# Edge counts scattered in BF16 under a bound computed on the chip, with an FP32 recount in a branch, and the first graph convolution summed from three BF16 parts

## The chip, the cores and the metric

The kernel runs on one core of a Trainium2 chip, in one launch. The metric is device time in microseconds (us) of that launch. The core has five engines with queues of their own: TensorE (PE, with its weight loads listed as PEld), VectorE (DVE), ScalarE (ACT), GpSimd (POOL) and SyncE (SP), which here issues nearly all plain transfers. GpSimd issues the indirect ones, those that add into memory and those that convert a type. Sixteen DMA engines carry all of them. P is 128, the number of partitions.

## The reference

3,125 nodes with 256 features, 100,000 edges (`src`, `dst`, sorted by `dst`), and 65,536 edges of a second graph (`edge_index` of the mixture stage). What matters here is cut from two layers:

```python
def segment_sum(src, seg, n): return jax.ops.segment_sum(src, seg, n)
xn = layernorm(x)
# layer 0, graph convolution
agg = segment_sum(xn[src], dst, N)
h = (xn + agg) @ W.T + b                        # then batch norm over the nodes
x = x + h_normed + linear_attention_stack(xn)   # four layers
# layer 0, second part: graph attention over edge_index picks experts
x = x + experts(layernorm(x), edge_index)
# layer 1: the same edges src, dst, twice
xn = layernorm(x)
h = (1 + eps1) * xn + segment_sum(xn[src], dst, N)
h = relu(relu(h @ W1a + b1a) @ W1b + b1b)
h = (1 + eps2) * h + segment_sum(h[src], dst, N)
x = x + relu(h @ W2a + b2a) @ W2b + b2b + attention(xn)
x = x + mixture_of_experts(layernorm(x))
```

The kernel writes a segment sum as a matrix product. It counts for every pair of nodes how many edges go from the one to the other, which makes a matrix of 3,125 x 3,125, and multiplies the features by it on TensorE. The matrix of `src`, `dst` is used three times; that of the second graph, C, is used in the graph attention.

## The kernel before

**Counting the edges.** Each edge gets a key, `src * N + dst` as FP32, which is its place in the matrix. 128 edges make a column, one per partition: 782 columns for list a (`src`, `dst`) and 512 for list b (the second graph). The columns are taken in windows: for list a 1, 7 and then 8 columns wide up to column 88, and from there 5 and 4 wide in turn, by chunks of at most 32 columns (`chunks_of`, L236). The last chunk is filled up to whole windows; edges that fill a list carry source 0 and destination N, and BAD = 2^24 is added to their keys.

`Edges.prepare` (L311) works out the values on VectorE. For each column of a window one instruction (L343) compares its keys with all keys of the window; equal keys that stand earlier weigh BEFORE = 4096 and all others 1, and the sum goes into `val`. So the first edge of a key gets the number of edges with that key in the window, and the others get at least 4096. A few short instructions (L353 to L357) then replace by an unused place (`dump`) the index of an edge that is not the first of its key, or that only fills the list. `scatter` (L390) issues one indirect transfer on GpSimd for each column, which adds the 128 values to the matrix in memory. Within a window no place occurs twice, so the program is told that those scatters need not wait for each other (L402), and each scatter of a window waits for those of the window before (L405). `both` (L413) sets the order: from column 88 a window of list a and two columns of list b in turn; what is left of list b, 198 columns in windows of 16 (TAIL), is scattered last. Before that, SP clears both matrices (`clear`, L454): AT for list a, C2 for list b, each in FP32, 25 transfers each.

This is spread over the four attention layers of layer 0: `beside` (L537) lets `both` run on a step after every tile of 128 nodes.

**First graph convolution.** After the layers, xn is loaded again (L700). `aggregate` (L657) goes over the matrix in two passes, of three and of four groups of 512 columns. For each of 25 row tiles SP loads a slice of AT in FP32 (L673), VectorE takes its maximum into `most` (L675), and TensorE multiplies xn by it in FP32 (L680); the first tile also adds xn itself by the identity (L688). `done0` brings the sums to SBUF, multiplies them by the weights and collects batch norm statistics. Beside this, GpSimd still scatters the last columns of list b. The next stage, graph attention, loads C from L880 on.

**The branch flag.** In the graph attention's second pass the maximum is brought together over the partitions, and `more` becomes 1 if it is over MOST = 256 (L923 to L926). In the same pass GpSimd copies AT to A1 in BF16, in 25 transfers spread over the pass (`copy_counts`, L929).

**Layer 1.** Integers to 256 are exact in BF16. `sums` (L1406) multiplies the features, split into three BF16 parts (`parts`, L1397), by A1. For counts over 256 there is `residue` (L1436): for 7 groups of columns and 25 row tiles it loads a slice of AT and of A1, each into a tile with one buffer, forms what A1 lacks in two further BF16 parts with four VectorE operations, and multiplies the three parts of the features by both. It stands in a branch (`if_more`, L1459), once after the first sum (L1595, two blocks of 128 features) and once before the second (L1650, four blocks). A branch is a unit: nothing from inside runs beside what is outside.

Of the kernel before, what the change touches and what calls it, by code (L numbers as in the profile page):

```python
# [17 lines left out]
P = 128  # L18
N = 3125
# [65 lines left out]
def tile_gps(ctx: ExitStack, tc: tile.TileContext, a, out):  # L85
# [207 lines left out]
    class Edges:  # L293
# [7 lines left out]
        def __init__(self, ep, w_before, dump, key, width, used, rows, mat, tag):  # L301
# [7 lines left out]
            self.ps = None  # L309

        def prepare(self, cols, win):  # L311
# [7 lines left out]
            for c in range(c0, c1, win):  # L319
# [20 lines left out]
                for j in range(k):  # L340
                    junk = ep.tile([P, WIDE * P], BF16, name="junk", tag="junk", bufs=2)
# [15 lines left out]
            V.tensor_tensor(idx, rel[:, :w], dump[:, :w], op=OP.add)  # L357
            yield

        def prepare_tail(self, c, k):  # L360
# [9 lines left out]
            for j in range(k):  # L370
                for i, (h, w) in enumerate(halves):
                    junk = ep.tile([P, WIDE * P], BF16, name="junk", tag="junk", bufs=2)
# [17 lines left out]
        def scatter(self, c, end, other=None):  # L390

            if c < self.used:
# [3 lines left out]
                    in_=self.val[:, c:c + 1], in_offset=None, compute_op=OP.add)  # L396
# [16 lines left out]
    def both(ea, eb, clear_b):  # L413
# [36 lines left out]
    with ExitStack() as st:  # L450
# [3 lines left out]
        def clear(mat):  # L454

            m = mat.rearrange("(p b f) -> p b f", p=P, f=CLR // 4)
            for b in range(25):
                nc.sync.dma_start(m[:, 4 * b:4 * b + 4, :], zero[:, None, :].to_broadcast([P, 4, CLR // 4]))
                yield
# [10 lines left out]
        first, later = clear(AT), clear_own()  # L470
# [5 lines left out]
        steps(first, 4)  # L476
        with tc.tile_pool(name="ps_keys", bufs=1, space=PSUM) as ps:
            key_a = keys(ep, ps, a["src"], a["dst"], E0, True, "a")
            steps(first, 3)
# [35 lines left out]
        ea = Edges(ep, w_before, dumpf, *key_a, AT, "a")  # L515
        behind = both(ea, Edges(ep, w_before, dumpf, *key_b, C2, "b"), later)
# [140 lines left out]
    def aggregate(ps, ap, X, nfb, self_id, passes, done, most, shared):  # L657


        for groups in passes:  # L660
            c0, c1 = 512 * groups[0], min(N, 512 * (groups[-1] + 1))
            bank, acc = None, {}
            for i, g in enumerate(groups):
                if g == shared:
                    bank = ps.tile([P, nfb, P], F32, name="agb", tag="agb", bufs=1)
                for fb in range(nfb):
                    acc[fb, i] = (bank[:, fb, :] if g == shared else
                                  ps.tile([P, 512], F32, name=f"ag{fb}_{i}", tag=f"ag{fb}_{i}", bufs=1))
            for s in range(NT):
                r = rows_of(s)  # L670
                ch = ap.tile([P, 512 * 3 + cols_of(NG - 1)], F32, name="ch", tag="ch", bufs=3)
                for q0, q1 in split_rows(r):
                    nc.sync.dma_start(ch[q0:q1, :c1 - c0], AT2[s * P + q0:s * P + q1, c0:c1])  # L673
                at = passes.index(groups) * NT + s
                V.tensor_reduce(most[:r, at:at + 1], ch[:r, :c1 - c0], axis=AX.X, op=OP.max)  # L675
                for fb in range(nfb):
                    w = X[:r, s, fb * P:(fb + 1) * P]
                    for i, g in enumerate(groups):
                        n = cols_of(g)
                        T.matmul(acc[fb, i][:, :n], lhsT=w, rhs=ch[:r, i * 512:i * 512 + n],  # L680
                                 start=s == 0 and (g != shared or fb == 0),
                                 stop=s == NT - 1 and (g != shared or fb == nfb - 1), skip_group_check=g == shared)
                if s == 0:
                    for fb in range(nfb):
                        for i, g in enumerate(groups):
                            for j, t in enumerate(tiles_of(g)):
                                q = rows_of(t)
                                T.matmul(acc[fb, i][:, j * P:j * P + q], lhsT=X[:q, t, fb * P:(fb + 1) * P],  # L688
                                         rhs=self_id[:q, :q], start=False, stop=False, skip_group_check=g == shared)
            for i, g in enumerate(groups):  # L690
                for fb in range(nfb):
                    done(i, g, fb, acc[fb, i], cols_of(g))
# [3 lines left out]
    most_p = ctile([P, 1], "most_p")  # L696
    more = ctile([1, 1], "more", I32)
    with ExitStack() as st:
        gp = st.enter_context(tc.tile_pool(name="gnn0", bufs=1))
        xn = gp.tile([P, NT, D], F32, name="xn", tag="xn")  # L700
        for g in range(NG):
# [1096 lines left out]
```

## Time and profile before

| what | value |
|---|---|
| median of 3 runs | 5,089.27 us (5,079.68 to 5,099.22) |
| the profiled execution's own time | 5,094.23 us |
| its span, first to last instruction | 5,092.4 us |
| PE busy | 4,003.0 us, 79% |
| DVE busy | 3,218.2 us, 63% |
| POOL busy | 2,769.6 us, 54% |
| ACT busy | 1,467.1 us, 29% |
| DMA, mean | 104 GB/s |

The span cut into 40 equal slices shows where which engine is busy; a digit is the share in tenths, and PEclk is the granted TensorE clock in tenths of full speed. A slice is 127 us:

```profile
PE   1457888878766877849979964666689998999999
PEld 1234455445544454524446641222245444544477
DVE  7978887898899874113348996889973031331231
ACT  0311133114111321200014448989740021000033
POOL 0668888888888888877760006888620031001034
PEclk6668888889787878969989986888899999999999
DMA  9954444444332322247656536543291212212266
```

The first 17 or 18 slices are the attention layers with the scatters of the edges on POOL, slices 18 to 21 the first convolution and the batch norm, then up to slice 29 the graph attention, then layer 1 and the experts. The costliest groups are listed by line with the number of instructions, their busy time in us, the mean of one in ns, and the idle time of the engine just before them with what ended it. In order of time, a row has its start and length in us, engine and line, what it writes and reads, and in brackets the idle time before it and what ended that.

### The profile page before, as it was taken

The numbers are of one execution on the slowest core, as the hardware profiler recorded it, in microseconds if no ns is written. First come the engines' busy times: TensorE is split into PE (matmuls) and PEld (weight loads), VectorE is DVE, ScalarE is ACT, GpSimd is POOL, SyncE is SP. The second block draws the span as 40 slices with busy tenths as digits, with TensorE's granted clock in tenths as the row PEclk, the third lists the DMA queues.
The fourth block names the chain that finished last, engine by engine and source line by source line (L and its number), as shares of the span: only waits on it lengthen the run. The fifth ranks groups of instructions, "written<-read, shape, count | busy, mean of one in ns | idle before, by whom it ended". The sixth has DMA issues, their size and how long they took to land. (4 is left out here: it accounts for less than half of the span.)

```text
span 5092.4 us, 48980 instructions
## 1 busy us (share of the span) xinstructions
PE 4003.0 (79%) x16189; PEld 2300.3 (45%) x16189; DVE 3218.2 (63%) x8074; ACT 1467.1 (29%) x2293; POOL 2769.6 (54%) x1860
## 2 busy tenths in 40 slices
PE   1457888878766877849979964666689998999999
PEld 1234455445544454524446641222245444544477
DVE  7978887898899874113348996889973031331231
ACT  0311133114111321200014448989740021000033
POOL 0668888888888888877760006888620031001034
PEclk6668888889787878969989986888899999999999
DMA  9954444444332322247656536543291212212266
GB/s 371 329 117 74 83 72 55 81 79 56 26 26 17 34 16 1 5 88 138 131 101 216 186 123 176 138 121 104 84 280 55 83 50 70 64 54 68 57 170 169
DMA packets 457112, 530.76 MB, mean 104 GB/s; under 512 B 213682, under 2 KB 354779, under 8 KB 451798
## 3 DMA queue, kind: packets, MB, share of 16 engines
q1 hardware_dynamic: 256058, 494.24, 30.7%
q0 software_dynamic: 200784, 33.23, 13.9%
q8 instruction: 133, 2.18, 0.2%
q14 instruction: 137, 1.11, 0.1%
HBM read 397.41 MB, written 169.95 MB: 111 GB/s over the span
## 5 line engine op out<-in xcount | busy, mean ns | idle before, releaser
L394 POOL DMA_INDIRECT AT<-vala,keya x782 | 1232.6, 1576 | 421.0 <-issue 221.0
L394 POOL DMA_INDIRECT C<-valb,keyb x512 | 807.6, 1577 | 203.4 <-issue 143.0
L988 POOL TENSOR_TENSOR ex<-ex,pqb 128x1024 f32<-128x1024 f32 (+3 forms) x200 | 367.0, 1857 | 434.0 <-ACT ex L987 433.4
L343 DVE SCALAR_TENSOR_TENSOR junk<-kr,keya,w_before 128x640 bf16<-128x640 f32 (+2 forms) x729 | 573.1, 830 | 0.6 <-DMA kr<-keys_a 0.6
L383 DVE SCALAR_TENSOR_TENSOR junk<-kr,keyb,w_before 128x1024 bf16<-128x1024 f32 (+1 forms) x390 | 482.3, 1269 | 4.5 <-DMA kr<-keys_b 4.4
L194 PE MATMUL tr<-ident,rows 128*128 128x128 f32 (+1 forms) x500 | 103.4, 361 | 465.8 <-ACT rows L180 441.0
L228 PE MATMUL mm<-hT,w 128*128 128x512 f32 (+1 forms) x896 | 418.2, 632 | 17.2 <-ACT hT L196 16.9
L1430 PE MATMUL ag<-chb,Hb 128*128 128x512 bf16 (+1 forms) x1800 | 420.1, 387 | 13.0 <-DMA chb<-A 13.0
L887 DVE CUSTOM_DVE_ANT_0 am<-asb,pen 128x1664 f32<-128x1664 f32 (+3 forms) x200 | 357.3, 1786 | 51.0 <-ACT pen L884 41.0
L649 PE MATMUL o<-w,hid 128*128 128x256 f32 (+1 forms) x1600 | 383.0, 393 | 0.0
L1023 PE MATMUL pa<-ex,hgp 128*32 128x512 f32 (+3 forms) x1400 | 208.4, 676 | 197.1 <-DVE ex L1011 193.9
L1011 DVE SCALAR_TENSOR_TENSOR ex<-ex,ct 128x2048 f32<-128x2048 f32 (+3 forms) x175 | 345.7, 2007 | 23.4 <-ACT ex L1004 13.8
L1004 ACT ACTIVATE ex<-ex,as 128x1024 f32<-128x1024 f32 (+3 forms) x400 | 345.2, 932 | 3.4 <-DVE ex L993 2.9
L649 PEld LDWEIGHTS o<-w,hid 128*128 128x128 f32 (+1 forms) x1600 | 296.9, 190 | 79.4 <-issue 34.7
L1259 POOL DMA_INDIRECT slots<-rb,r_ati x50 | 49.8, 997 | 516.2 <-DVE rb L1252 407.6
L680 PE MATMUL ag<-ch,xn 128*128 128x512 f32 (+1 forms) x600 | 272.5, 602 | 62.3 <-issue 62.3
L231 ACT ACTIVATE hid<-mm,fm 128x512 f32<-128x512 f32 (+1 forms) x336 | 211.1, 632 | 370.4 <-PE mm L228 353.0
L228 PEld LDWEIGHTS mm<-hT,w 128*128 128x128 f32 x896 | 191.7, 233 | 234.9 <-issue 190.0
L194 PEld LDWEIGHTS tr<-ident,rows 128*128 128x128 f32 (+1 forms) x500 | 66.7, 174 | 506.6 <-ACT rows L180 469.2
L180 ACT ACTIVATE rows<-xs,ln_nmr,rs_y 128x256 f32<-128x256 f32 (+1 forms) x200 | 105.7, 592 | 649.0 <-DVE ln_nmr L173 625.1
L1430 PEld LDWEIGHTS <-Hb 128*128 128x128 bf16 (+1 forms) x2100 | 184.9, 99 | 226.9 <-issue 35.1
L675 DVE TENSOR_REDUCE most<-ch 128x1 f32<-128x1536 f32 (+3 forms) x50 | 89.0, 1780 | 228.7 <-DMA ch<-AT 228.5
(430 smaller groups left out, 6962.5 us busy)
## 6 DMA issues: line engine op xcount, KB each, us to landing
AT<-zero SPq DMA_DIRECT2D x25, 1528.0 KB
C<-zero SPq DMA_DIRECT2D x25, 1528.0 KB
cnt<-C SPq DMA_DIRECT2D x24, 1562.5 KB
cd<-C SPq DMA_DIRECT2D x36, 1024.0 KB
kr<-keys_b SPq DMA_DIRECT2D x64, 512.0 KB
f1w<-in_f_w_dram SPq DMA_DIRECT2D x56, 512.0 KB
slots<-blank SPq DMA_DIRECT2D x15, 1820.0 KB
kr<-keys_a SPq DMA_DIRECT2D x48, 512.0 KB
```

Source lines behind the costliest of these rows:

```text
L228: T.matmul(ph[:, :n], lhsT=w1[:, k, hb * P:(hb + 1) * P], rhs=xT[:, k, :n], start=(k == 0), stop=(k == 1))
L231: S.activation(h[:, :n], ph[:, :n], AF.Gelu, bias=bias[hb])
L343: V.scalar_tensor_tensor(junk[:, :k * P], self.kr[:, at:at + k * P], key[:, c + j:c + j + 1], self.w_before[:, u:u + k * P], op0=OP.is_equ ...
L383: V.scalar_tensor_tensor(out, kk, key[:, c + j:c + j + 1], by, op0=OP.is_equal, op1=OP.mult, accum_out=more[:, j:j + 1] if i else self.val ...
L394: s = G.indirect_dma_start(out=self.flat, out_offset=bass.IndirectOffsetOnAxis(ap=self.idx[:, c:c + 1], axis=0), in_=self.val[:, c:c + 1], ...
L649: T.matmul(po[:r], lhsT=hid[hb][:, j * P:j * P + r], rhs=w2[:, hb, :], start=(hb == 0), stop=False)
L680: T.matmul(acc[fb, i][:, :n], lhsT=w, rhs=ch[:r, i * 512:i * 512 + n], start=s == 0 and (g != shared or fb == 0), stop=s == NT - 1 and (g ...
L887: V.tensor_tensor_reduce(out=junk[:r, :w], in0=asb[:r, h, c0:c1], in1=pen[:r, :w], scale=1.0, scalar=-3.0e38, op0=OP.subtract, op1=OP.max, ...
L988: G.tensor_tensor(e, e, pq[:r, h, :n], op=OP.add)
L1004: S.activation(ex[:r, h, :n], ex[:r, h, :n], AF.Exp, bias=sc)
L1011: V.scalar_tensor_tensor(e4, e4, 1.0, ct[:r, None, :m].to_broadcast([r, 4, m]), op0=OP.min, op1=OP.mult)
L1430: T.matmul(acc[fb, g][:, :n], lhsT=Xb[:r, s, i, fb * P:(fb + 1) * P], rhs=ch[:r, at:at + n], start=first, stop=last, skip_group_check=g == ...
```

## The change

- A1, the matrix in BF16, takes the place of AT in the first counting: it is cleared (in 20 transfers) and list a is scattered into it, from `low`, a BF16 copy of the values that ACT makes in `prepare`.
- For each window of list a, `prepare` takes the largest value under BEFORE into a column of `most`, on each partition. `at_most` takes the maximum over the partitions by two transposes and adds up all windows; `more` is 1 if that is over MOST = 256. It is set before the first convolution.
- If `more` is 1, `recount` clears AT, scatters list a once more in FP32 into it and copies it to A1, and `residue` adds what A1 lacks. For the recount no scatter is declared independent of another.
- The first convolution is done by `sums`, from three BF16 parts of xn; these are made by ACT and, for the differences, TensorE. `sums`, `residue` and `parts` move up in the text. `aggregate`, the maximum over AT and the copies in the graph attention's second pass are removed.
- The last 198 columns of list b are no longer scattered by `both`; they are kept in `tail` and scattered after the branch.
- `junk` has one buffer in place of two. aT starts at zero and is added to.

```diff
         def __init__(self, ep, w_before, dump, key, width, used, rows, mat, tag):
...
+            self.low = None
+            if mat.dtype == BF16:
+                self.low = ep.tile([P, width], BF16, name=f"low{tag}", tag=f"low{tag}")
+                self.most, self.windows = ep.tile([P, 2 * P], F32, name=f"most{tag}", tag=f"most{tag}"), 0
+                V.memset(self.most, 0.0)
         def prepare(self, cols, win):
...
+            if self.low is not None:
+                S.activation(self.low[:, c0:c1], val, AF.Copy)
+                n = w // win
+                V.scalar_tensor_tensor(rel[:, :w], val, BEFORE, val, op0=OP.is_lt, op1=OP.mult)
+                V.tensor_reduce(self.most[:, self.windows:self.windows + n],
+                                rel[:, :w].rearrange("p (n w) -> p n w", w=win), axis=AX.X, op=OP.max)
+                self.windows += n
...
-                    in_=self.val[:, c:c + 1], in_offset=None, compute_op=OP.add)
+                    in_=(self.val if self.low is None else self.low)[:, c:c + 1], in_offset=None, compute_op=OP.add)
...
+        def at_most(self, ps):
+            top = small.tile([P, 2], F32, name="e_top", tag="e_top")
+            for i in range(2):
+                p = ps.tile([P, P], F32, name="mt", tag="mt", bufs=2)
+                T.transpose(p, self.most[:, i * P:(i + 1) * P], ident)
+                V.tensor_reduce(top[:, i:i + 1], p, axis=AX.X, op=OP.max)
+            p = ps.tile([P, P], F32, name="mt", tag="mt", bufs=2)
+            for i in range(2):
+                T.matmul(p[:1, :1], lhsT=top[:, i:i + 1], rhs=ones_col, start=(i == 0), stop=(i == 1))
+            return p[:1, :1]
+        def recount(self, zero, mat, low):
+            f = CLR // 4
+            m = mat.rearrange("(p b f) -> p b f", p=P, f=f)
+            for b in range(25):
+                nc.sync.dma_start(m[:, 4 * b:4 * b + 4, :], zero[:, None, :].to_broadcast([P, 4, f]))
+            for c in range(self.used):
+                G.indirect_dma_start(
+                    out=mat.rearrange("(n o) -> n o", o=1),
+                    out_offset=bass.IndirectOffsetOnAxis(ap=self.idx[:, c:c + 1], axis=0),
+                    in_=self.val[:, c:c + 1], in_offset=None, compute_op=OP.add)
+            for b in range(25):
+                G.dma_start(out=low.rearrange("(p f) -> p f", p=P)[:, CLR * b:CLR * (b + 1)],
+                            in_=mat.rearrange("(p f) -> p f", p=P)[:, CLR * b:CLR * (b + 1)])
...
-                eb.scatter(c, (c - c0) % TAIL == TAIL - 1 or c == eb.made - 1)
+                tail.append((c, (c - c0) % TAIL == TAIL - 1 or c == eb.made - 1))
...
-        ea = Edges(ep, w_before, dumpf, *key_a, AT, "a")
+        ea = Edges(ep, w_before, dumpf, *key_a, A1, "a")
...
+        S.activation(aT, ones_col[:, 0:1, None].to_broadcast([P, 2, N]), AF.Copy, scale=0.0)
...
+            V.tensor_scalar(more, ea.at_most(ps), MOST, None, op0=OP.is_gt)
+            for t in range(NT):
...
+                S.activation(xb[:r, t, 0, :], x, AF.Copy)
+                for i in range(2):
+                    p = ps.tile([P, D], F32, name="rest", tag="rest", bufs=6)
+                    T.matmul(p[:r], lhsT=ident[:r, :r], rhs=x, start=True, stop=False)
+                    for k in range(i + 1):
+                        T.matmul(p[:r], lhsT=less[:r, :r], rhs=xb[:r, t, k, :], start=False, stop=(k == i))
+                    S.activation(xb[:r, t, i + 1, :], p[:r], AF.Copy)
+        with (tc.tile_pool(name="g0t", bufs=1) as rp, tc.tile_pool(name="ps_g0t", bufs=1, space=PSUM) as ps,
+              if_more()):
...
+            ea.recount(zero, AT, A1)
+            residue(ps, rp, xb, 2, add0)
+        for c, end in tail:
+            eb.scatter(c, end)
...
-            aggregate(ps, gp, xn, 2, ident, [[0, 1, 2], [3, 4, 5, 6]], done0, most, NG - 1)
+            sums(ps, gp, xb, 2, [[0, 1, 2], [3, 4, 5, 6]], done0, shared=NG - 1, own=ident_b)
...
-                if s % 3 == 2:
-                    copy_counts(state.get("gone"))
-                    state["gone"] = o
```

More of the change, by code (lines that the diff above doesn't have):

```diff
@@ L469, in tile_gps @@
         V.memset(each, 1.0)
-        first, later = clear(AT), clear_own()
+        first, later = clear(A1), clear_own()
         def steps(it, n):
@@ L1459, in if_more @@
-    def if_more():
-        return tc.If(nc.values_load(more[0:1, 0:1], min_val=0, max_val=1,
-                                    skip_runtime_bounds_check_because="the result of a comparison") > 0)
     with ExitStack() as st:
```

190 lines of the change are left out of this document (80 added, 110 removed).

## The prediction

> **What bounds the kernel now.** I read the page's costliest groups first, then the busy time by stretches, then GpSimd in order of time where the first graph stage begins.
>
> ```profile
> L394 POOL DMA_INDIRECT AT<-vala,keya x782 | 1232.6, 1576 | 421.0 <-issue 221.0
> L394 POOL DMA_INDIRECT C<-valb,keyb x512 | 807.6, 1577 | 203.4 <-issue 143.0
> L680 PE MATMUL ag<-ch,xn 128*128 128x512 f32 (+1 forms) x600 | 272.5, 602 | 62.3 <-issue 62.3
> ```
>
> Until 2,250 us GpSimd scatters edges, 1.58 us each and one after the other: the two lists together hold it for 2,040 us of busy time. In the stretch 1,950 to 2,100 us it is busy 125.5 of 150 us, which is 81 scatters, one per 1.86 us. The layers' own work ends at 2,197 us and the first aggregation (L680) waits until 2,260 for the last scatter.
>
> ```profile
> 2243.92 1.55 POOL L394 DMA_INDIRECT AT<-vala,keya  x1 [0.30 <-issue]
> 2247.45 1.55 POOL L394 DMA_INDIRECT AT<-vala,keya  x1 [1.97 <-DMA AT<-vala,keya]
> 2249.31 1.55 POOL L394 DMA_INDIRECT C<-valb,keyb  x1 [0.30 <-issue]
> 2251.17 1.55 POOL L394 DMA_INDIRECT C<-valb,keyb  x1 [0.30 <-issue]
> ```
>
> The second line is the one to keep: the last scatter of list a may not run beside the one before it, and starts 3.53 us after it (2247.45 - 2243.92) where its neighbours follow in 1.86.
>
> **The question that decides: is the branch taken?** Before, `more` compared the largest real count with 256; the largest is 3, and the residue's lines (L1446 to L1457) have no row in the trace. Now `more` compares a bound: for each window the largest multiplicity in it, summed over all windows. From `chunks_of`: 782 columns of 128 edges make 12 + 157 = 169 windows. The edges are sorted by destination, 32 per node, so a window of 5 columns holds 20 nodes and 20 x (32 x 31 / 2) / 3125 = 3.2 expected pairs with equal source: nearly every window has a duplicate. Counted on the reference's `src` and `dst`, of the first 168 windows 11 have the maximum 1, 156 have 2 and one has 3: 11 + 312 + 3 = 326. That alone is over 256. The last window adds more: the last chunk is 15 columns for 12, so 96 + 3 x 128 = 480 filler edges carry one and the same key; the first of them gets the value 480, which is under BEFORE = 4096 and passes the new filter. Sum 326 + 480 = 806 > 256. So `more` is 1, and all three branches run: the recount with its residue in stage 0, and both residues of layer 1, which so far are skipped.
>
> **The work added, part by part.** All three bodies stand alone: nothing else is in flight to hide them.
>
> (1) Clearing AT: 25 transfers of 1,528 KB, 39.1 MB. The same clears run now between 20 and 100 us at a mean 386 GB/s: 101 us.
>
> (2) The recount's 782 scatters. Here no scatter is declared independent of the one before, as L402 and L1262 do for theirs, so each waits for its predecessor to land. Rows for that: 3.53 us above, 3.27 at 361.05 us; beside large loads 4.1 to 6.1 (the C windows after 2,257 us). Nothing runs beside the recount, so 3.53: 782 x 3.53 = 2,760 us. Ends: 1.86 if no wait is set (1,455) and 5.8 (4,536). Behind each waiting scatter stand the next ones, the copies and C's last scatters on GpSimd; for the copies wait SP's residue loads, and for these DVE and PE, so the wait is paid in full.
>
> (3) 25 copies AT to A1 with the cast. In 3,300 to 3,520 us the software queue, which then carries only these copies, takes 16.8% of 220 us for 6.71 of 19.5 MB, 8.6 copies: 4.3 us each, 108 us; at most some 7 us each if each waits for the last. I take 115.
>
> (4) One residue step, 7 groups x 25 tiles of them. With one buffer for each load, a step is a chain: last matmul, load of the BF16 slice, four DVE operations, matmuls.
>
> ```profile
> 2268.51 0.37 SPq L207 DMA_DIRECT2D xg<-in_x_dram  x1
> 2271.07 1.23 DVE L743 TENSOR_TENSOR xs<-xs,xg 128x1024 f32<-128x1024 f32 x1 [2.78 <-DMA xg<-in_x_dram]
> L1538 DVE TENSOR_TENSOR kv<-kv,kv_by 128x512 f32<-128x512 f32 x24 | 16.8, 743 | 0.2
> 23.78 0.62 DVE L275 CAST dfa<-dia 128x896 f32<-128x896 int32 x1
> 4254.07 0.61 PE L1430 MATMUL ag<-chb,Hb 128*128 128x512 bf16 x1
> 4254.47 0.25 PE L1430 MATMUL agb<-chb,Hb 128*128 128x53 bf16 x1
> 4256.05 0.38 PE L1430 MATMUL ag<-chb,Hb 128*128 128x512 bf16 x1
> 4256.26 0.19 PE L1430 MATMUL agb<-chb,Hb 128*128 128x53 bf16 x1
> ```
>
> A load of 512 KB lands 2.56 us after its issue; for 128 KB I take 2.2 (1.6 to 2.6). Two subtractions at 0.74 and two casts at 0.62 x 512/896 = 0.36 make 2.2 (2.9 if a cast costs the 0.69 of L200). A BF16 matmul of 512 columns steps in 0.40 us after idle time (4254.47 - 4254.07) and in 0.21 once PE has been busy for 4.7 us. Each step leaves PE some 4 us idle, and after 3.02 us idle at 3,313.66 eight matmuls of L1023 take 1.93 us, later 1.07; so I price the first 12 of a step at 0.40. One matmul starts before the last cast, so 11 x 0.40 = 4.4. Hand-overs between the engines 0.5 (1.0). Sum 9.3 us with two feature blocks; with four, 11 x 0.40 + 12 x 0.21 = 6.9, sum 11.8. Groups of 53 columns: 4.4 and 5.6 us. So 150 x 9.3 + 25 x 4.4 = 1,505 us twice, and 150 x 11.8 + 25 x 5.6 = 1,910, with 80 for adding the seven results: 5,000 us. Ends: 6.6 and 9.1 a step (3,670), 11.3 and 15.7 (6,150).
>
> The Trainium skill (TensorE: Matmul & The Clock Gate, What's actually happening) says that PE falls to half rate only after a whole idle window of about 3.4 us, and that the windows run freely. An idle time of 4 us seldom covers one, so by that rule most steps would stay at 0.21 and cost 7.2 and 9.7: some 4,100 us in all. The row at 3,313.66, slow after 3.02 us, is nearer, and I keep it.
>
> (5) The branch itself. In the skipped one at L1595 the compare takes 0.05 us on ACT and 3.83 on PE, which has to jump; the bodies now follow in line. 15 us for the three (0 to 40).
>
> **The rest of the change.** Clearing BF16 A1 moves 19.5 MB less: GpSimd, whose first scatter stands until 113.9 us behind the clears, starts some 50 us earlier and ends near 2,200. A BF16 scatter has as many descriptors, so I take the same 1.58; the queues have fourfold slack (23.4% of 150 us for 81 scatters), and L1259's scatter of 1.0 is the lower end; DVE, busy 137 of 150 us in 1,500 to 1,650, would take over as the bound. The bound itself, two DVE and one ACT operation for 33 chunks at 0.16 to 0.3 us, is hidden under that; uncovered it would be some 30 us. One buffer for junk in place of two costs nothing, since DVE writes it in order and nobody reads it. After 2,197 us the split of xn follows: loads 4, the zeroed aT 6, 75 ACT casts of 0.41 = 31, so the branch opens near 2,245. The sums in BF16 replace 315 us of FP32 by 900 x 0.21 + 150 x 0.07 = 200 us and some 15 of evictions. But the last 198 scatters of C, which now run beside the aggregation (2,257 to 2,669 us, 412 in all), are queued behind the branch. The stage after, which loads C at 2,675, needs them: 2,245 + 412 + 5 against 2,675 saves 15, however fast the sums are. 25 copies leave the attention stage, where PE to POOL waits of 30 us went with them, but its bound is ACT (134 to 140 of 150 us): 10.
>
> **Sum** on the profiled execution's own 5,094 us (span 5,092; the median of the runs, 5,089, is 0.1% less): 5,094 + 101 + 2,760 + 115 + 5,000 + 15 - 25 = 13,060 us; I say 13,050.
>
> **Rivals.**
> A, the branch is not taken (some step of my count is wrong, a filler edge or a comparison): then 5,094 + 5 (three skipped branches, one more than now) - 25 - 10 (the shorter sums, as far as C's scatters let them show) = 5,064 us, faster by 0.6%. For it: no row shows how the values are weighted, my count rests on reading the code. Against it: 326 without any filler edge. This is the case on the other side; it decides wherever the sum is at most 256.
> B, the recount's scatters are not chained: 782 x 1.86 = 1,455 in place of 2,760, 11,750 us. For it: all 1,294 scatters now go at 1.86. Against: they do because the code says for each that it may.
> C, a chained scatter takes the 5.8 us of the C windows: 782 x 5.8 = 4,536, 14,830 us. Against it: those ran beside loads of 768 KB, and had up to 16 scatters in front.
>
> **Chances.** Forecast 0.72, A 0.06, B 0.12, C 0.10. The forecast's own ends: residues 3,670 with scatters at 3.27 gives 11,530; residues 5,800 with scatters at 3.8 gives 14,070. The range 11,200 to 14,300 takes in most of B and the lower part of C. A measurement of this kernel can tell about 0.5% from no change, and A lies about there, so it is split in halves: faster 0.03, same 0.03, slower 0.94.
>
> **What would show it.** Right: rows for the recount's scatters, 782, some 3.5 us apart with the wait on their own predecessor; matmuls of the residue, 2,100 + 2,100 + 4,200; a step near 9 to 12 us; C's last scatters after the branch. Wrong: no row in the recount's lines (A); a period of 1.86 (B); residue steps under 6 us, where loads and matmuls of two steps overlap after all.

## The result, and the profile after

| | us |
|---|---|
| before, median of 4 runs | 5,094.25 (5,079.68 to 5,100.98) |
| changed kernel, median of 4 runs | 12,244.35 (12,241.84 to 12,247.77) |
| ratio, with its 95% interval | 2.405 (2.401 to 2.410) |
| span of the profiled execution, before and after | 5,092.4 and 12,246.1 |
| predicted | 13,050 (11,200 to 14,300) |

The branch is taken, all three times. The forecast had the direction and the mechanism, and was 6.6% too long. Four of the costliest groups of the changed kernel (busy us and mean ns of one, then idle time just before and what ended most of it):

```profile
L768 PE MATMUL re<-re_b,xb 128*128 128x512 bf16 (+2 forms) x4128 | 1507.3, 524 | 4052.2 <-DVE re_b L764 4043.9
L763 DVE TENSOR_TENSOR re_c<-re_c,re_b 128x512 f32<-128x512 f32 (+2 forms) x1050 | 655.3, 624 | 6010.5 <-DMA re_b<-A 5992.4
L446 POOL DMA_INDIRECT AT<-vala,keya x782 | 1212.1, 1550 | 1393.0 <-DMA AT<-vala,keya 1332.9
L768 PE MATMUL re<-re_b,Hb 128*128 128x512 bf16 (+2 forms) x4128 | 1076.2, 426 | 610.1 <-DVE re_b L764 592.9
```

None of these lines ran before. The recount's 782 scatters (L446) wait for their own transfers, 1,333 us in all. The residue's chain can be read from the releasers: PE waits for the casts (L764), VectorE for the loads (`re_b<-A`). Its 5,992 us of waiting include the 2,825 us in which it only stood at the branch.

The busy time by stretches, cut at the events of the trace, shows the bill. The columns are us, then busy us with the number of instructions for PE, PEld, DVE, ACT and POOL, the granted clock, DMA share and GB/s:

```profile
2251.00:2366.00 115.00, 0.00 (x0) 0.00 (x0) 0.00 (x0) 0.31 (x1) 53.94 (x35) 0.51 1.06 349
2366.00:4936.00 2570.00, 0.00 (x0) 0.00 (x0) 0.00 (x0) 0.00 (x0) 1211.05 (x782) 0.50 0.13 0
4936.00:5043.00 107.00, 0.46 (x1) 0.22 (x3) 1.69 (x3) 0.00 (x0) 25.03 (x34) 0.50 0.94 187
5043.00:6437.00 1394.00, 754.48 (x2065) 254.70 (x2100) 364.78 (x713) 0.00 (x0) 208.93 (x133) 0.68 0.22 43
6437.00:6677.00 240.00, 232.41 (x1233) 109.43 (x1254) 23.82 (x37) 8.87 (x14) 0.00 (x0) 0.99 0.29 88
6677.00:8178.00 1501.00, 1174.65 (x5454) 616.08 (x5475) 1111.08 (x1590) 808.21 (x1095) 519.55 (x374) 0.87 0.40 129
8178.00:9553.00 1375.00, 752.59 (x2064) 253.51 (x2100) 366.36 (x719) 0.00 (x0) 0.00 (x0) 0.68 0.16 43
...
9704.00:11403.00 1699.00, 1076.52 (x4129) 438.39 (x4202) 373.56 (x732) 0.69 (x2) 2.85 (x5) 0.79 0.16 44
```

In order: clears, scatters, casts, the first residue, the sums of stage 0, the attention up to the end of layer 1's first sums, the second residue, and the third with its entry and the first load after it. The residue stretches have one thing in common: no engine is busy for more than two thirds of the time, and the granted clock is 0.68 to 0.79. In the 2,570 us of scatters nothing but GpSimd works, at less than half.

Set against before, the added parts are 115 + 2,570 + 107 + 1,394 + 1,375 + 1,686 = 7,247 us (the third residue without the 12.4 us of waiting for the first load after it). The difference of the spans is 7,154, so the rest of the kernel became 93 us shorter: GpSimd's list a ends at 2,187.8 instead of 2,247.5, which opens the branch 9 us before the old sums opened (2,251 against 2,260); the sums of stage 0 to their statistics take 240 instead of 314; the attention 1,501 instead of 1,509; a few us lie in the seams. The old sums' stretch, with 1 us of the statistics in it, for the row of 6,437 to 6,677 above:

```profile
2260.00:2575.00 315.00, 307.88 (x856) 146.76 (x856) 109.97 (x85) 12.58 (x21) 240.58 (x155) 0.99 0.67 130
```

One residue step, by the timeline (start, duration, engine; weight loads left out):

```profile
5503.10 0.32 SPq L761 DMA_DIRECT2D re_b<-A  x1
5505.26 0.69 DVE L763 TENSOR_TENSOR re_c<-re_c,re_b 128x512 f32<-128x512 f32 x1 [6.67 <-DMA re_b<-A]
5506.05 0.43 DVE L764 CAST re_b<-re_c 128x512 bf16<-128x512 f32 x1
5506.51 0.69 DVE L763 TENSOR_TENSOR re_c<-re_c,re_b 128x512 f32<-128x512 f32 x1
5506.53 0.59 PE L768 MATMUL re<-re_b,xb 128*128 128x512 bf16 x2 [3.46 <-DVE re_b L764]
...
5507.23 0.43 DVE L764 CAST re_b<-re_c 128x512 bf16<-128x512 f32 x1
5507.69 0.32 SPq L760 DMA_DIRECT2D re_c<-AT  x1
5507.71 3.63 PE L768 MATMUL re<-re_b,xb 128*128 128x512 bf16 x10 [0.59 <-DVE re_b L764]
...
5511.37 0.32 SPq L761 DMA_DIRECT2D re_b<-A  x1
```

From one load of the BF16 slice to the next: 2.16 us until VectorE starts (5505.26 - 5503.10), 2.40 of VectorE to the end of the second cast, 3.63 of ten matmuls, 8.27 in all with the hand-overs. Of the next step only the FP32 load (`re_c<-AT`, 5507.69) runs beside the matmuls; the load of the BF16 slice, on which VectorE waits, does not.

### The profile page after: what moved, and what is told of

Read it like the earlier page. It is cut to its first block, busy times and chain, and to the rows that moved or that the text cites. A ratio compares the mean times of both kernels' runs of the same rounds, so it can differ in the third digit from the quotient of the medians.

```text
span 12246.1 us, 73086 instructions
## 1 busy us (share of the span) xinstructions
PE 6576.3 (54%) x24933; PEld 3244.6 (26%) x25169; DVE 4298.1 (35%) x10253; ACT 1499.2 (12%) x2396; POOL 3970.9 (32%) x2642
## 4 chain that ended last, share of the span: by engine, by line
PE 43%; DMA 30%; DVE 20%; issue 4%; ACT 2%; SPq 1%; another core or an unknown queue 1%; POOL 1%; DVEq 0%; POOLq 0%; ACTq 0%
DMA AT<-vala,keya 19%; PE re L768 18%; DMA re_b<-A 9%; PE ag L737 6%; DVE re_c L763 5%; PE mm L228 4%; PE o L694 3%; DVE re_b L764 3%; DVE am L990 3%; DVE junk L349 2%; DVE ex L1100 2%; PE mm L609 1%; DVE junk L397 1%; PE o L220 1%; PE o L681 1%
## 5 line engine op out<-in xcount | busy, mean ns | idle before, releaser
L768 PE MATMUL re<-re_b,xb 128*128 128x512 bf16 (+2 forms) x4128 | 1507.3, 524 | 4052.2 <-DVE re_b L764 4043.9
L763 DVE TENSOR_TENSOR re_c<-re_c,re_b 128x512 f32<-128x512 f32 (+2 forms) x1050 | 655.3, 624 | 6010.5 <-DMA re_b<-A 5992.4
L768 PEld LDWEIGHTS <-xb 128*128 128x128 bf16 (+1 forms) x4200 | 508.3, 130 | 5051.7 <-issue 4985.9
L446 POOL DMA_INDIRECT AT<-vala,keya x782 | 1212.1, 1550 | 1393.0 <-DMA AT<-vala,keya 1332.9
L768 PE MATMUL re<-re_b,Hb 128*128 128x512 bf16 (+2 forms) x4128 | 1076.2, 426 | 610.1 <-DVE re_b L764 592.9
L408 POOL DMA_INDIRECT A<-lowa,keya x782 | 1228.4, 1571 | 370.5 <-issue 222.1
L768 PEld LDWEIGHTS <-Hb 128*128 128x128 bf16 (+1 forms) x4200 | 438.3, 115 | 1248.1 <-issue 982.0
L349 DVE SCALAR_TENSOR_TENSOR junk<-kr,keya,w_before 128x640 bf16<-128x640 f32 (+2 forms) x729 | 603.3, 828 | 10.5
L709 POOL TENSOR_TENSOR rest<-h1o,Hb 128x512 f32<-128x512 f32 (+1 forms) x25 | 28.9, 1155 | 1727.5 <-ACT Hb L708 1727.5
L764 DVE CAST re_b<-re_c 128x512 bf16<-128x512 f32 (+2 forms) x1050 | 413.1, 393 | 70.3 <-DVE re_c L763 0.2
L737 PE MATMUL ag<-chb,Hb 128*128 128x512 bf16 (+1 forms) x1752 | 417.2, 388 | 14.6 <-DMA chb<-A 12.4
L737 PE MATMUL ag<-chb,xb 128*128 128x512 bf16 (+2 forms) x1906 | 397.5, 365 | 3.9 <-DMA chb<-A 1.1
```

Of the source, the lines that this page charges most:

```text
L349: V.scalar_tensor_tensor(junk[:, :k * P], self.kr[:, at:at + k * P], key[:, c + j:c + j + 1], self.w_before[:, u:u + k * P], op0=OP.is_equ ...
L408: s = G.indirect_dma_start(out=self.flat, out_offset=bass.IndirectOffsetOnAxis(ap=self.idx[:, c:c + 1], axis=0), in_=(self.val if self.low ...
L446: G.indirect_dma_start(out=mat.rearrange("(n o) -> n o", o=1), out_offset=bass.IndirectOffsetOnAxis(ap=self.idx[:, c:c + 1], axis=0), in_= ...
L737: T.matmul(acc[fb, g][:, :n], lhsT=Xb[:r, s, i, fb * P:(fb + 1) * P], rhs=ch[:r, at:at + n], start=first, stop=last, skip_group_check=g == ...
L763: V.tensor_tensor(ch[:r, :n], ch[:r, :n], cb[:r, i, :n], op=OP.subtract)
L764: V.tensor_copy(cb[:r, i + 1, :n], ch[:r, :n])
```

## Experiments

Ratios are against runs of the kernel before on the same chip. The names are those of the expectations.

**Is it the bound that takes the branch, and what is left without the branch?** e1_not_taken changes one number of the changed kernel:

```diff
-MOST = 256.0
+MOST = 806.0
```

> The changed kernel with one number edited: the threshold is 806 in place of 256, so the three branches are skipped if the bound on the chip is the 806 that was counted by hand (what is left out with it: a count above 256 would no longer be recounted). Theory, the branch is all of the loss and C's scatters bound what is left: the list a ends at 2,188 as in the changed kernel, then 198 scatters of C at 2.1 to 2.2 us end near 2,616 (before 2,669), the attention stage saves 8, so 5,094 - 53 - 8 = 5,033 us (5,010 to 5,064), faster by 1.2%. Rival, the prediction's case A: 5,064. Second rival, the bound is over 806: then 12,244.

Measured: 5,074.28 us against 5,101.24, ratio 0.994 (0.993 to 0.995). The branch is skipped, so the sum on the chip is at most 806, and the branch is the whole of the loss. But the gain is that of the prediction's case A (27 us; it said 30), not the 61 expected here. The sums' first loads tell why:

```profile
2318.91 1.54 POOL L408 DMA_INDIRECT C<-valb,keyb  x1 [0.30 <-issue]
2324.69 1.54 POOL L408 DMA_INDIRECT C<-valb,keyb  x1 [4.24 <-DMA C<-valb,keyb]
...
2324.56 4.25 SPq L730 DMA_DIRECT2D chb<-A  x8
2327.77 6.24 PE L737 MATMUL ag<-chb,xb 128*128 128x512 bf16 x18 [67.20 <-DMA chb<-A]
```

PE, ACT and SP read `more` at 2,260; SP issues the loads only at 2,324.6, as GpSimd goes on after a pause. GpSimd read the flag at 2,308.3, and the pause follows six scatters later. The rows of the branch's own line on GpSimd's queue (count, ns of one, start) show that the pause is the passing of the branch:

```profile
L808 POOLq COMPARE_BRANCH  x1: 53/53/53, 2308.9 to 2308.9; - x1
L808 POOLq INC_SWDGE_SEM  x1: 1552/1552/1552, 2322.4 to 2322.4; - x1
```

The second of them, by its name an increment of a semaphore of the software DMA queue that carries the scatters, begins as the last scatter ahead of it lands (3.5 us after its start, by the median) and ends at 2,324.0, 0.6 us before SP's first load. The profile puts the last 56 us of SP's wait down to a landing of C, which goes by the same queue. GpSimd came late because part of C's last scatters stands in its queue ahead of the branch. So the shorter sums began 68 us later than the old ones and gained next to nothing.

**The largest count read back from A1 itself, in place of the summed bound.** e7_exact, cut to its core:

```diff
+                    for q0, q1 in split_rows(r):
+                        nc.sync.dma_start(ch[q0:q1, :c1 - c0], A12[s * P + q0:s * P + q1, c0:c1])
+                    at = i * NT + s
+                    V.tensor_reduce(most[:r, at:at + 1], ch[:r, :c1 - c0], axis=AX.X, op=OP.max)
...
-            V.tensor_scalar(more, ea.at_most(ps), MOST, None, op0=OP.is_gt)
+            V.tensor_scalar(more, ea.at_most(ps, gp), MOST, None, op0=OP.is_ge)
...
+        for c, end in tail:
+            eb.scatter(c, end)
         with (tc.tile_pool(name="g0t", bufs=1) as rp, tc.tile_pool(name="ps_g0t", bufs=1, space=PSUM) as ps,
```

> The summed bound is replaced by the largest count found in A1 itself, read back once after the scatters of list a, and the branch is taken from 256 on; C's last scatters are put ahead of the branch on GpSimd. The largest count is 3, so no branch runs. Reading back is 50 loads and 50 reductions of about 1.6 us, 83 us on VectorE, before the sums can open: 2,251 + 85 + 240 = 2,576, and C's scatters end near 2,616 in any case. Theory, the check hides under C's scatters: 5,033 us, the same as the run with threshold 806 within 10. Rival, the check lies on the path: 85 more than that run, 5,118, slower than before.

Measured: 5,268.84 us, ratio 1.033 (1.031 to 1.034): slower than before, and 195 us above e1 where the rival said 85. SP reads `more` at 2,325, 65 us later than in e1, but the sums waited another 200:

```profile
2526.29 1.54 POOL L400 DMA_INDIRECT C<-valb,keyb  x1 [4.74 <-issue]
...
2528.66 5.57 PE L736 MATMUL ag<-chb,xb 128*128 128x512 bf16 x18 [209.28 <-DMA chb<-A]
...
L809 POOLq INC_SWDGE_SEM  x1: 1458/1458/1458, 2523.7 to 2523.7; - x1
```

With more scatters ahead of it, GpSimd reads the flag at 2,508.7 and, seven scatters later, stands from 2,521.6 to 2,526.3 with no releaser in the profile; its increment ends at 2,525.2, and the first load of the sums is at 2,525.4. In e11 below, where the branch is skipped too, the two are at 2,322.1 and 2,322.6. The sums moved by 201 us with GpSimd's passing of the branch (2,528.7 - 2,327.8), and the whole kernel by 196. That is the wait both kernels share.

**How much of the bound comes from filler edges?** Three runs use the selection, which filler edges fail, in place of the test of the value alone, with `MOST` at 256 (e5), 326 (e6) and 328 (e11):

```diff
-                V.scalar_tensor_tensor(rel[:, :w], val, BEFORE, val, op0=OP.is_lt, op1=OP.mult)
+                V.tensor_tensor(rel[:, :w], val, sel[:, :w], op=OP.mult)
```

> Filler edges are left out of the bound, the threshold stays 256. Theory: the windows of real edges alone sum to 326, so all three branches still run: 12,244 us. Rival, the 480 of the filler edges are what takes the branch: 5,033.

Measured (one run): 12,290.54 us. The windows of real edges alone take the branch. The 46 to 50 us by which this run and the next are over the changed kernel were not taken apart.

> Filler edges are left out of the bound (the value is multiplied by the selection that their keys fail, in place of the test of the value alone), and the threshold is 326, exactly the sum counted by hand for the 168 windows of real edges plus nothing for the last (what is left out: counts from 257 to 326 would not be recounted). Theory: the bound is 326 or less, the branches are skipped, 5,033 us. Rival, the hand count is too low: 12,244.

Measured: 12,294.13 us, ratio 2.410 (2.406 to 2.413). The expectation was wrong: the count of 326 covered 168 windows, and the last window holds 160 real edges with a pair among them, so it adds 2.

> As the run with threshold 326, which was taken, but with 328: that count left out the last window, whose 160 real edges hold a pair, so it adds 2. Theory: the bound without filler edges is exactly 328, the branches are skipped, and the time is that of the run with threshold 806, 0.994 of before, 5,070 us. Rival, the count has another error: 12,290.

Measured (one run): 5,073.42 us. Skipped at 328 and taken at 326: with sums of whole numbers the bound without filler edges is 327 or 328, and the hand count says 328.

**The recount's chain of waits.** e2_unchained declares the scatters of a window independent, as list a's are:

```diff
             for c in range(self.used):
-                G.indirect_dma_start(
+                s = G.indirect_dma_start(
...
+                if not first and not last:
+                    for o in started:
+                        tc.declare_no_dep(s.ins, o.ins, reason="no index twice in a window")
+                if not first:
+                    for o in before + (started if last else []):
+                        tc.add_manual_dep(s.ins, o.ins.name, self.after, reason="the window before")
```

> The recount's scatters are declared independent within a window, as the scatters of list a are; each window still waits for the one before. Theory, the 1.7 us that each of the 782 waits for its predecessor's landing is the term: 782 x 1.86 = 1,455, plus one wait of 1.43 (3.29 - 1.86) for each of 168 windows, 240, makes 1,695 in place of 2,570: 11,370 us (11,130 to 11,500). Rival, the rate is set by the queue or the memory and not by the wait: 12,244.

Measured: 11,456.22 us, ratio 2.250 (2.246 to 2.254), 788 less than the changed kernel. The scatters run from 2,370.3 to 4,139.8, 2.27 us each. First two of the chained ones of the changed kernel, then a window of e2:

```profile
4925.66 1.55 POOL L446 DMA_INDIRECT AT<-vala,keya  x1 [1.68 <-DMA AT<-vala,keya]
4928.93 1.55 POOL L446 DMA_INDIRECT AT<-vala,keya  x1 [1.72 <-DMA AT<-vala,keya]
```

```profile
3310.51 1.55 POOL L449 DMA_INDIRECT AT<-vala,keya  x1 [2.21 <-DMA AT<-vala,keya]
3312.36 1.55 POOL L449 DMA_INDIRECT AT<-vala,keya  x1 [0.30 <-issue]
```

The wait is the term: 1.7 us for each scatter there, here 1.7 to 2.2 for each window. It falls short of the 875 expected because a window's wait costs 1.89 us on average, (1,769.5 - 781 x 1.86) / 168, not 1.43.

**The residue's single buffers.** e3_two_bufs; the second residue stays as it is and serves as a control:

```diff
-    def residue(ps, ap, Xb, nfb, add):
+    def residue(ps, ap, Xb, nfb, add, n_c=1, n_b=1):
...
-                ch = ap.tile([P, 512], F32, name="re_c", tag="re_c", bufs=1)
-                cb = ap.tile([P, 3, 512], BF16, name="re_b", tag="re_b", bufs=1)
+                ch = ap.tile([P, 512], F32, name="re_c", tag="re_c", bufs=n_c)
+                cb = ap.tile([P, 3, 512], BF16, name="re_b", tag="re_b", bufs=n_b)
...
-            residue(ps, rp, xb, 2, add0)
+            residue(ps, rp, xb, 2, add0, 1, 2)
...
-                residue(ps, rp, Hb, 4, add2)
+                residue(ps, rp, Hb, 4, add2, 2, 2)
```

> The residue's tiles get more buffers: in stage 0 two of re_b and one of re_c, in the residue with Hb two of each; the residue with xb in layer 1 stays as it is. Theory, a step is a chain because of the single buffers, and PE is slow because the chain leaves it idle: stage 0 goes from 8.7 us a step to load 2.2 + VectorE 2.4 = 4.6, 780 us in place of 1,394; Hb goes from 10.5 to PE at full rate, 24 x 0.21 = 5.1, 840 in place of 1,680; the third stays at 1,375. Sum 12,244 - 614 - 840 = 10,790 us (10,700 to 10,950). Rival, PE's slow rate doesn't come from the idle time: Hb stays at 24 x 0.43 = 10.3 a step, 1,600, and stage 0 takes 5.1, 850: 11,620.

Measured: 10,987.66 us, ratio 2.158 (2.154 to 2.162). First matmul to the next part: 897 us in stage 0 (1,394 in the changed kernel), 1,375 in the control (1,375), 925 with Hb (1,690). The rows of the three residues, in this order, by stretches of 100 us:

```profile
5500.00:5600.00 100.00, 71.72 (x228) 26.40 (x232) 44.03 (x79) 0.00 (x0) 0.00 (x0) 0.83 0.27 73
8600.00:8700.00 100.00, 57.01 (x141) 18.62 (x142) 25.18 (x46) 0.00 (x0) 0.00 (x0) 0.70 0.17 47
9700.00:9800.00 100.00, 94.45 (x418) 41.22 (x425) 41.25 (x75) 0.00 (x0) 0.00 (x0) 1.00 0.30 88
```

Where PE has work waiting the clock is 1.00 and a step with 24 matmuls takes 5.7 us (24 in 418 per 100 us); in the chain it stays at 0.70. The rival falls. Stage 0 gained less than expected because with two of `re_b` and one of `re_c` the FP32 load is on the chain, and it lands 2.7 us after its issue, not 2.16.

**Both together.** 

> Both edits together, the unchained recount and the residue with more buffers. Theory, the terms stand alone and add up: 12,244 - 875 - 1,454 = 9,915 us, and in any case the sum of the two runs' gains within 40. Rival, C's last scatters on GpSimd, 300 us beside the residue of stage 0, become its bound: no gain lost below 300 us of residue, so this would show only as a tail after it.

Measured: 10,188.10 us, ratio 2.002 (1.998 to 2.006). The gains of the two runs, 788 + 1,257 = 2,045, make 2,056 together: the terms stand alone. Even the cheaper branch doubles the time.

**What the clock costs.** e9_no_split leaves the four VectorE operations out of each step and multiplies by the rounded counts, so its sums are not the residue. e12_filled adds matmuls that nobody reads:

```diff
+                for _ in range(18 if nfb == 2 else 16):
+                    T.matmul(fill, lhsT=Xb[:, 0, 0, 0:P], rhs=Xb[:, 0:512 // Xb.shape[-1], 1, :], start=True, stop=True)
```

> The residue's four VectorE operations are left out of every step, and its matmuls take the rounded count itself, so a step is load and matmuls alone and PE is idle for some 2.3 us between steps where it was idle 3.5 and 0.6. Theory, any idle time of 2 us or more brings back the slow rate for about 3 us: 8 matmuls at 0.43, 4 at 0.21 and 2.3 make 6.6 us a step with two feature blocks, 9.1 with four: 12,244 - 2 x 150 x 2.1 - 150 x 1.4 = 11,400 us. Rival, PE stays at full rate over so short an idle time: 12 x 0.21 + 2.3 = 4.9 and 7.4 a step: 12,244 - 300 x 3.8 - 150 x 3.1 = 10,640.

Measured (one run): 11,193.30 us. The first residue takes 1,039 us and the third 1,316, between the two expectations: neither slow again after every idle time of 2 us nor at full rate throughout. What decided between them is in the last section.

> Work is added: behind the matmuls of every residue step 18 more (16 with four feature blocks) on operands that lie ready, into a PSUM tile that nobody reads, so PE has next to no idle time. Theory, the clock of a window follows how busy PE was in the window before, so PE stays at full rate and a step is load 2.16 + VectorE 2.40 + 10 x 0.216 + 0.1 = 6.8 us in place of 8.7, and 8.7 in place of 10.5: 12,244 - 300 x 1.9 - 150 x 1.8 = 11,400 us. Rival, the slow matmuls come from something else (the operands' landing, weights' loading): each step gets 18 x 0.43 = 7.7 us more PE work, of which the load hides some 3.5: 12,244 + 450 x 4.2 = 14,100.

Measured: 11,876.02 us, ratio 2.330 (2.326 to 2.334): 368 less with more work. In stage 0 the order of the queue put all 3,150 added matmuls ahead of the residue, in the time of the recount, so there the step stayed as it was, and only the other two residues were filled:

```profile
5500.00:5600.00 100.00, 57.87 (x141) 18.80 (x143) 26.56 (x48) 0.00 (x0) 0.00 (x0) 0.68 0.16 44
8300.00:8400.00 100.00, 99.19 (x439) 43.19 (x444) 32.88 (x59) 0.00 (x0) 0.00 (x0) 1.00 0.21 56
9750.00:9850.00 100.00, 98.77 (x441) 43.28 (x448) 24.91 (x44) 0.00 (x0) 0.00 (x0) 1.00 0.22 62
```

439 matmuls at 30 a step are one step in 6.83 us, as expected for full rate (6.8), where the unfilled chain takes 8.6; with Hb 441 at 40 a step are 9.1 us (10.5 unfilled). Of the 476 us by which the expected 11,400 is missed, 285 are the unfilled stage 0, 60 a delay of 0.4 that the filling puts on each step with Hb, and 46 a recount that ended later in this execution (4,981 against 4,935); the remaining 85 were not taken apart.

**The layer-1 residues alone.** e4_before_taken is the kernel before with `MOST = 2.5`.

> The kernel before with the threshold 2.5 in place of 256: the largest count is 3, so its two layer-1 branches run, and nothing else of the change is in it. Theory, the two residues cost there what they cost in the changed kernel, 1,375 + 1,686 = 3,061: 5,094 + 3,061 = 8,155 us (8,120 to 8,190). Rival, their price depends on the stage 0 of the changed kernel (its recounted A1 or its queues): off by more than 100.

Measured (one run): 8,147.84 us against 5,112.98 (one run), 3,035 more. In the changed kernel the two residues take 1,375 + 1,686 = 3,061, so they cost the same without the rest of the change, within 1%.

**A version that is faster than both.** e10_after_sums, cut to its core:

```diff
                     nc.sync.dma_start(ch[q0:q1, :c1 - c0], A12[s * P + q0:s * P + q1, c0:c1])
+                if most is not None:
+                    at = passes.index(groups) * NT + s
+                    V.tensor_reduce(most[:r, at:at + 1], ch[:r, :c1 - c0], axis=AX.X, op=OP.max)
...
+            sums(ps, gp, xb, 2, [[0, 1, 2], [3, 4, 5, 6]], add0, shared=NG - 1, own=ident_b, most=most)
...
+            V.tensor_scalar(more, most[0:1, 0:1], MOST, None, op0=OP.is_ge)
         with (tc.tile_pool(name="g0t", bufs=1) as rp, tc.tile_pool(name="ps_g0t", bufs=1, space=PSUM) as ps,
               if_more()):
-            ea.recount(zero, AT, A1)
+            ea.recount(zero, AT)
             residue(ps, rp, xb, 2, add0)
+        with tc.tile_pool(name="ps_g0y", bufs=1, space=PSUM) as ps:
+            for g in range(NG):
```

> The check moves behind stage 0's sums: VectorE takes the largest count of each loaded slice of A1 beside the matmuls, the branch follows the sums and is taken from 256 on, its body no longer writes A1 (the casts are gone; the residue of all three places is the true count minus what A1 holds, in two BF16 parts). With the largest count 3 no branch runs. In the run with threshold 806 the sums' loads stood until 2,324 us, when GpSimd had passed the branch, because the body's casts would write A1; here nothing that follows reads what GpSimd would write. Theory: sums from 2,263 for 219 us, 3 for the largest, 5 for the branch, 14 blocks of 1.9 us, the statistics at 2,520 (2,567 in the run with 806, 2,574 before), attention masks from 2,632 behind C's last scatters at 2,618 (before 2,682), 8 less in the attention: 5,092 - 50 - 8 = 5,034 us, faster than before by 1.1% (5,020 to 5,060). Rival, something else than the casts held the loads, an exit of the branch that all engines share: then the statistics wait for GpSimd behind C's scatters, some 2,640, and the time is 5,150.

Measured: 5,018.22 us against 5,100.69, ratio 0.985 (0.983 to 0.987). The products with wg and the statistics for all seven groups stand behind the branch. Of the reads of the flag, by line, the lines give count, ns of one (least, median, most), and the starts of the first and the last:

```profile
L754 SPq TENSOR_LOAD <-more x3: 282/483/539, 2469.4 to 4172.3; - x3
...
L754 POOLq TENSOR_LOAD <-more x3: 294/299/507, 2615.0 to 4173.2; - x3
```

PE's next work, by the timeline, is 4.6 us behind the first of them, although GpSimd comes to the branch only at 2,615:

```profile
2474.01 2.04 PE L811 MATMUL py<-aT,wg 128*128 128x512 f32 x2 [5.14 <-PEq L802]
```

So an exit that all engines share is excluded. The masks of the attention start at 2,625.1, before at 2,682.4; they now follow C's last scatter at 2,615.2 directly, which is the next bound of this stage.

## Why the prediction was right, and where its sizes were off

**The branch.** Right: the sum of window maxima takes it (e1, e5). The count of 326 missed the 2 of the last window's real edges, which changes nothing: the 480 of the filler edges is that window's maximum.

**(1) Clears, 101 us.** 115: the transfers are issued in 98 us, and the first scatter waits until the last one has landed, which the term left out.

**(2) Scatters, 782 x 3.53 = 2,760 us.** The mechanism is shown by e2. The size was 2,570, a period of 3.29 ((4935.5 - 2366.3) / 781). Of the two rows named, 3.27 would have been nearly right. Both were single waits among free scatters, none in a chain, and why the one took 3.53 is not shown. This is 190 of the error.

**(3) Casts, 115 us.** 107. Their pace is 3.64 us each, and the first residue load waits out the landing of the last, 29 us.

**(4) Residues, 5,000 us.** 1,394 + 1,375 + 1,686 = 4,455; this is 545 of the error, and the term that was most off. A step was put at 9.3 us with two blocks and took 8.7 and 8.6 (without 25 short steps of 3.5); with four it was put at 11.8 and took 10.5. The load (2.16 against 2.2) and VectorE (2.40 against 2.2) were close. Two pieces were not. The hand-overs take under 0.1 us, not 0.5. And with two blocks ten matmuls, not eleven, are left behind the last cast, and in both kinds of step some of the first 12, which the prediction priced at 0.40, run at 0.21: the matmuls take some 4.1 us of a step instead of 4.4 with two blocks, and 5.9 instead of 6.9 with four. The 80 for adding the results lies inside the measured steps. The ends of 3,670 and 6,150 don't say what a short step costs in them; with 4.4 and 5.6 they come to 3,785 and 6,185. That the slow rate comes from PE's idle time was right as a trend only: the last section shows that it goes by the work of a whole window. The row at 3,313.66 was no clean sign of it either, as the same eight matmuls took 1.70 us at 3,308.34 with no wait just before them. By the Trainium skill (TensorE: Matmul & The Clock Gate, What's actually happening) the sum was 4,100, too low by 355; what the runs show of its rule stands in the last section.

**(5) Branches 15, the rest -25, together -10.** -93. The step that failed: "the last 198 scatters of C, which now run beside the aggregation ... are queued behind the branch", with the stage priced as 2,245 + 412 + 5. That is the price without the branch. With it taken, 58 of the 198 ran ahead of the recount, from 2,204.6 to 2,332, and 140 behind it, from 5,016 to 5,317, nearly all beside the first residue, where GpSimd has nothing else to do. So these bodies did not stand alone: GpSimd went on to work behind the branch while the other engines were still inside it, against what the description of the kernel before says of a branch. They bound nothing any more, so the shorter sums gained their whole 74 us. The other half of the claim, GpSimd done some 50 us earlier, holds: 60.

**The sum.** 190 + 545 + 83 (rest) + 8 (casts) - 14 (clears) = 812, of 13,060 - 12,246 = 814 us.

**The rivals.** A (branch not taken, 5,064 us, 30 less than before) has the right size: e1 is 27 less. Its reason was not right: C's scatters were to bound the stage, but the sums did, held up until GpSimd had passed the branch. B and C on the scatters' pace are excluded by the period of 3.29.

**Open.** The loads of the sums go out 0.3 to 0.6 us after GpSimd's increment in e1, e7 and e11. That they are tied to it because the body's casts would write A1 fits these runs and e10, but e10 moved the branch and removed the casts at once, so which of the two freed the sums was not tried apart. Of the 74 us that e10's span is shorter, 57 lie ahead of the masks; the remaining 17 were not taken apart.

## What to carry to other kernels

Before pricing a fast path with a fallback, work out on real data whether its test passes: a bound that adds a maximum for each of 169 windows is over 256 with a largest count of 3, and the fallback is then the kernel. Read the test from the finished data beside work that is there anyway, and put the branch where no engine with a long queue has to pass it before others can go on. A chain of load, VectorE and matmuls through single buffers costs more than its parts, since it keeps PE's clock down as well.

## What the runs showed of the hardware

**The clock lags by a window, and goes by how much work the window held.** In the changed kernel the granted clock changes only on a grid of 3.41 us that stays fixed through the execution. Seven windows of that grid in the first residue (the first busy time is PE's, the third column from the end is the clock, mixed by a few hundredths at the cuts):

```profile
5493.60:5497.01 3.41, 0.39 (x2) 0.10 (x1) 0.73 (x2) 0.00 (x0) 0.00 (x0) 0.96 0.15 38
5497.01:5500.43 3.42, 2.80 (x7) 0.94 (x7) 1.51 (x3) 0.00 (x0) 0.00 (x0) 0.50 0.23 44
5500.43:5503.84 3.41, 2.63 (x7) 0.78 (x6) 0.00 (x0) 0.00 (x0) 0.00 (x0) 0.54 0.09 33
5503.84:5507.25 3.41, 0.59 (x2) 0.19 (x2) 1.82 (x4) 0.00 (x0) 0.00 (x0) 0.96 0.14 38
5507.25:5510.67 3.42, 2.96 (x8) 1.11 (x8) 0.41 (x1) 0.00 (x0) 0.00 (x0) 0.54 0.31 81
5510.67:5514.08 3.41, 0.67 (x4) 0.20 (x2) 0.58 (x1) 0.00 (x0) 0.00 (x0) 0.96 0.15 38
5514.08:5517.49 3.41, 2.53 (x6) 0.80 (x6) 1.66 (x4) 0.00 (x0) 0.00 (x0) 0.50 0.14 22
```

Full clock is granted in the window after a busy one, and in this chain that window is the one in which PE waits for the load. Over 199 such windows from 5,401 us on, 73 of 76 at full clock follow a window with PE busy for 2.8 us or more, and 117 of 123 at half clock follow one with 2.6 or less. The 76 windows that led to full clock were all at half clock themselves. Two of the nine exceptions stand in the rows above: 2.80 was followed by half clock and 2.63 by full. A window at full clock needs less busy time to keep it, as e9 shows, where these windows hold more work. The first row kept full clock; the window after the second was granted 0.51:

```profile
5423.78:5427.19 3.41, 1.90 (x9) 0.87 (x9) 0.00 (x0) 0.00 (x0) 0.00 (x0) 1.00 0.41 115
5427.19:5430.61 3.42, 1.30 (x6) 0.48 (x5) 0.00 (x0) 0.00 (x0) 0.00 (x0) 0.99 0.60 151
```

Over 199 windows there, the 18 at full clock that kept it held 1.43 to 2.11 us, and 81 of the 84 that lost it held 1.42 or less. At 0.43 us a matmul at half clock and 0.21 at full, 2.6 and 1.43 us are both six to seven matmuls, an estimate of where the line lies. It has exceptions: in the residue with Hb 19 of 163 windows at half clock with 2.8 us or more were followed by half clock again, which these runs don't explain. The lag is why the same ten matmuls take 3.63 us in one step and 4.43 in the next, and why adding matmuls (e12) made the kernel 368 us faster. The Trainium skill (TensorE: Matmul & The Clock Gate, What's actually happening) lets the clock fall after an idle window of about 3.4 us; the length and the free running agree with the grid here, but windows at full clock with up to 1.04 us of matmuls in them, 1.70 in e9, were followed by half clock too.

**A skipped branch can hold up other engines.** In e1 and e7 the loads behind a skipped branch went out within 1 us of the increment with which GpSimd passed it, 64 and 200 us after their own engine had read the flag, while in e10 the work behind it needed 5 us.

**A scatter that waits for its predecessor costs 3.29 us where nothing else runs**, 1.55 on GpSimd and 1.74 until it may go on; a free one follows in 1.86.
